# A three-layer feature-interaction network on one core: q of the first four chunks by pairs

## The chip, the cores and the metric

The kernel runs on one core of a Trainium2 chip. The metric is device time in microseconds (us), the median of several executions. Engines are named as the profile names them: PE (TensorE, matmul), PEld (its weight loads), DVE (VectorE), ACT (ScalarE), POOL (GpSimd), SP (the queue that issues most DMAs).

## The reference

```python
# x: (1024, 64, 16), W0, W1, W2: (128, 64*64)
h = x
for i in range(3):
    z = einsum('bfe,bge->bfge', x, h).reshape(B, 64 * 64, 16)
    y = einsum('oc,bce->boe', W[i], z) + b[i][None, :, None]
    x_i, h = (y[:, :64], y[:, 64:]) if i < 2 else (y, y)
    xs.append(x_i)
pooled = sum(concatenate(xs, axis=1), axis=2)      # over the 16 of e
out = pooled @ fc_w.T + fc_b                        # (1024, 1)
```

## The kernel before

All is fp32. The batch of 1024 is cut into 32 chunks of 32 rows. A chunk is a matrix of 64 features by 512 columns (32 rows times 16 of e).

**Algebra.** Products of x with itself are symmetric, so each pair of features (f, g) is made once, and the weights of (f, g) and (g, f) are added beforehand. The products of a chunk lie in 16 tiles z of 128 rows by 512 columns, made by VectorE in four instructions of four tiles each (`product`, L213, on line 217). The last group of four has one part (32 rows of its first tile) that holds squares, made by ScalarE (L222); the other 32 squares of a chunk are not in these tiles. From the same 16 tiles two 64-row results come: h1, the hidden half of layer 0, and q, a quadratic form of x that layer 2 and the output weights turn into (its weights m are built from W1 and W2 at run time). To q also belong the 32 other squares and a linear term, V1 x. The output of a chunk is the sum over e and features of uu0 = (h1 + bias) * q and uu1 = (V0 x + cx) * x, plus a constant.

**Weights.** `w_all` holds for each tile t 64 columns for h1, 64 for q, and 64 for h1 again (columns 128 to 191), so that an even chunk takes columns 0 to 127 (h1, q) and an odd one 64 to 191 (q, h1). `w_sq` is the same for the 32 other squares, four times below each other in row groups of 32. `v1w` is V1's weights, `bd` a block diagonal matrix of V0 (64 rows twice). q's weights come late: they are built by a chain of matmuls and sent through DRAM with DMAs into `ms`, and added by `q_weights`. So the first four chunks, `HEAD = [2, 3, 0, 1]`, are treated otherwise: h1 alone is made of them during the set-up, with `half_contract(c, 0, j)` (L286): 64 output rows, the columns 0 to 255 on one half of PE's columns and 256 to 511 on the other, side by side, into one accumulator of 128 rows by 256. `keep_h1` (L309) adds the squares to h1 of all four and ScalarE keeps h1 + bias in `hb`, in the same halves.

**q of the first four, before the change.** Chunks 0 and 1 are the last of the four; their z (`KEPT`) are still there when q's weights come, and `half_contract(c, 1, j)` makes their q at once (L545 to L548). Chunks 2 and 3 are loaded and multiplied a second time, within the main loop. The 17th tile, `zl`, made by ScalarE (`squares`, L224, and two copies in `last_tile`, L228), holds all 64 squares of the chunk and x itself; its weights in `w_all[:, NT]` are the first 32 squares' q weights, zeros, and V1. `half_contract(c, 1, NJ)` contracts it for each chunk. `v0x(k)` (L345) is a full 128x128 matmul of `bd` with the two chunks' x (`xx`). `factors` (L327) multiplies q with `hb`, in two pieces of 256 columns for each of these chunks.

**The other 28 chunks.** `contract(c, j)` (L254) makes h1 and q of a chunk with 16 full matmuls of 128x128 weights and 512 columns. After every second chunk of four, `contract_shared` (L263) adds what is missing to all four chunks: the squares, four matmuls of 32 rows in PE's four row groups, side by side; and for each pair of chunks V1 x and V0 x, four matmuls of 64 rows and 64 columns on the four quarters of PE.

**Order.** The program is in the order in which it is written (a manual schedule): each engine executes its instructions in that order, and waits by semaphores that are placed from the data and the buffers. The main loop (L629) goes over `order = [4, 5, 6, 7, 2, 3, 8, ..., 31]`; at step s it issues the loads and products of the chunk two steps ahead, contracts the present one, and has VectorE do the factors and sums of earlier ones. Chunks 4 and 5 are loaded before the loop. After chunk 4 the biases' constants and V0's weights are made (`biases`, `v0_weights`).

**Buffers.** x as loaded (`xa`, `xb`) has 3 buffers each, z has 12 (three chunks), `xx` 4, `zl` and the squares 4, `uu` 2. PSUM has 8 banks: tag "acc" 4, "y" 2, "set" 2. Buffers go round in turn.

Of the kernel before, what the change touches and what calls it, by code (L numbers as in the profile page):

```python
# [62 lines left out]
def cin_kernel(ctx, tc, xra, xrb, wh, w0r, w1h, w2t, wx1, wx0, vec, out):  # L63
# [11 lines left out]
    def const_tile(name, shape):  # L75
        return const.tile(shape, F32, tag=name, name=name)
# [49 lines left out]

    w_all = const_tile("w_all", [128, NT + 1, 192])
    w_sq = const_tile("w_sq", [128, 192])  # L130
    v1w = const_tile("v1w", [128, F])
    nc.gpsimd.memset(w_all[:, NT, :], 0.0)


    xas, xbs, zls, xxs, sqs = {}, {}, {}, {}, {}

    def load_xa(c, at=slice(0, NI)):
        if c not in xas or at.start == 0:
# [14 lines left out]
    def load_chunk(c):  # L153
        load_xa(c)
        load_xb(c)
# [40 lines left out]


    acc = const_tile("acc", [128, 2, NCH // 2, CB])
    hb = const_tile("hb", [128, NF, N // 2])
    accs, uus, zs, ys, parts = {}, {}, {}, {}, {}  # L200

    def new_acc(c, n=N, tag="acc"):
# [18 lines left out]
        if j == NJ - 1:  # L221
            nc.scalar.activation(zs[c, j][SQ, 0, :], xas[c][SQ, 0, :], AF.Square)  # L222

    def squares(c):  # L224
        zls[c] = xp.tile([128, N], F32, tag="zl", name=f"zl_{c}", bufs=4)
        nc.scalar.activation(zls[c][0:64], xas[c][0:64, 0, :], AF.Square)

    def last_tile(c):  # L228

        if c < FIRST:  # L230
            squares(c)
            nc.scalar.copy(zls[c][64:128], xas[c][64:128, 0, :])
        else:
            if c % 4 == 0:
                sqs[c // 4] = xp.tile([128, N], F32, tag="zl", name=f"sq_{c}", bufs=4)
            at = 32 * (c % 4)
            nc.scalar.activation(sqs[c // 4][at : at + 32], xas[c][0:32, 0, :], AF.Square)  # L237
        if c % 2 == 0:
            xxs[c // 2] = sp.tile([128, N], F32, tag="xx", name=f"xx_{c}", bufs=4)
        to = halves[c % 2]  # L240
        nc.scalar.copy(xxs[c // 2][to], xas[c][to, 0, :])  # L241

# [20 lines left out]
    def contract_shared(first):  # L263

        for r in range(4):
            c, at = first + r, slice(32 * r, 32 * r + 32)
            for acc_c, cols in pieces(c):
                nc.tensor.matmul(  # L268
                    acc_c, w_sq[at, w_cols(c)], sqs[first // 4][at, cols], start=(r >= 2),
                    stop=(r < 2), tile_position=(32 * r, 0),  # L270
                )
        for k in (first // 2, first // 2 + 1):
            ys[k] = ps.tile([128, N], F32, tag="y", name=f"y_{k}")
            for n in range(2):
                c, rows, q = 2 * k + n, halves[n], halves[1 - n]
                for acc_c, cols in pieces(c):
                    nc.tensor.matmul(  # L277
                        acc_c[q], v1w[rows], xxs[k][rows, cols], start=False, stop=(c % 4 < 2),
                        skip_group_check=True,
                    )  # L280
            for rows in halves:
                nc.tensor.matmul(ys[k][rows], bd[rows, rows], xxs[k][rows], start=True, stop=True)  # L282

    def half_contract(c, part, j):  # L286

        cols = slice(part * F, (part + 1) * F)
        for t in (NT,) if j == NJ else [j * NI + i for i in tiles(j)]:
            z = zls[c] if t == NT else zs[c, j][:, t % NI, :]  # L290
            for n in range(2):
                nc.tensor.matmul(  # L292
                    accs[c][halves[n]], w_all[:, t, cols], z[:, n * H2 : (n + 1) * H2],
                    start=(t == 0), stop=(t == NT),
                )


    sq_head = xp.tile([128, N], F32, tag="zl", name="sq_head", bufs=4)
    h1_accs = {}

    def head_square(c):
# [7 lines left out]
    def keep_h1():  # L309
        for r, c in enumerate(HEAD):  # L310
            at = slice(32 * r, 32 * r + 32)
            for n in range(2):
                nc.tensor.matmul(  # L313
                    h1_accs[c][halves[n]], w0ds[at], sq_head[at, n * H2 : (n + 1) * H2],
                    start=False, stop=True, tile_position=(32 * r, 64 * n),
                )
        for c in HEAD:
            nc.scalar.activation(
                hb[:, HEAD.index(c), :], h1_accs[c], AF.Identity, bias=bh1
            )  # L320

    def uu_tile(k):
# [4 lines left out]
    def factors(c, which=slice(0, 1)):  # L327

        uu = uu_tile(c // 2)[halves[c % 2], 0, :]
        if c in HEAD:  # L330
            for n in range(2):
                at = halves[n]
                nc.vector.tensor_tensor(
                    uu[:, n * H2 : (n + 1) * H2], accs[c][at], hb[at, HEAD.index(c), :], ALU.mult
                )
            return
        h = halves[c % 2]
        for acc_c, cols in pieces(c)[which]:
            q = sp.tile([128, N], F32, tag="q", name=f"q_{c}_{cols.start}")
            nc.scalar.copy(q[h, cols], acc_c[64 - h.start : 128 - h.start])  # L340
            nc.vector.scalar_tensor_tensor(  # L341
                uu[:, cols], acc_c[h], bh1[h], q[h, cols], ALU.add, ALU.mult
            )

    def v0x(k):  # L345
        ys[k] = ps.tile([128, N], F32, tag="y", name=f"y_{k}")
        nc.tensor.matmul(ys[k], bd, xxs[k], start=True, stop=True)  # L347

    def x_v0x(k):
        nc.vector.scalar_tensor_tensor(uu_tile(k)[:, 1, :], ys[k], cx, xxs[k], ALU.add, ALU.mult)  # L350
# [35 lines left out]
    nc.vector.memset(w0o[3][SQ, 0, :], 0.0)  # L386
    for j in (2, 3):
        h1_weights(j, w0o[j])
    half_contract(c0, 0, 0)


    head_acc(c1)
# [8 lines left out]
    product(c0, 3)  # L401
    load_chunk(c3)
    for j in range(1, NJ):
        half_contract(c0, 0, j)


    for j in range(NJ - 1):
# [13 lines left out]
            )  # L421
        nc.scalar.copy(v2r[:, n, :], pv)

    half_contract(c1, 0, 0)


    pt = ps.tile([128, F // 4, 4], F32, tag="y", name="pt")
# [2 lines left out]
        for to in halves:  # L430
            nc.tensor.matmul(pt[to, q, :], v2q[:, q, :], pick, start=True, stop=True)  # L431
    nc.scalar.copy(v2t, pt.rearrange("p q k -> p (q k)"))
    half_contract(c1, 0, 3)


    m_sb = z_tile("m_sb")
# [9 lines left out]
        nc.scalar.copy(m_sb[:, m, :], pms[m])  # L446

    for j in (1, 2):
        half_contract(c1, 0, j)

# [25 lines left out]
    for j in range(NJ):  # L476
        product(c2, j)
    for j in range(NJ):
        half_contract(c2, 0, j)


    ms = set_tile("ms").rearrange("p (v t g) -> p v t g", v=2, g=F)
# [31 lines left out]
    for j in range(NJ):  # L514
        product(c3, j)
    for j in range(NJ):
        half_contract(c3, 0, j)

    for j in range(1, NJ):
        for half in range(2):  # L520
# [14 lines left out]
    for j in range(NJ):  # L535
        q_weights(j)
    nc.vector.tensor_copy(w_all[SQ, (NJ - 1) * NI, 64:128], dg[SQ])
    nc.vector.tensor_copy(w_all[0:32, NT, 64:128], w_sq[0:32, 64:128])

    nc.scalar.copy(w_all[:, 0:NT, 128:192], w_all[:, 0:NT, 0:64])  # L540
    for to in (slice(0, 64), slice(128, 192)):
        nc.scalar.copy(w_sq[:, to], w0ds)


    for c in KEPT:  # L545
        new_acc(c, H2, "y")
        for j in range(NJ):
            half_contract(c, 1, j)  # L548

    made = set()  # L550

# [24 lines left out]
    for to in halves:  # L576
        for n in range(2):
            nc.vector.tensor_copy(v1w[to, 32 * n : 32 * n + 32], v1h[halves[n]])
    nc.scalar.copy(w_all[64:128, NT, 64:128], v1w[64:128])

    load_products(FIRST + 1)

# [12 lines left out]
    cst = const_tile("cst", [2, 1])  # L595

    def biases():
        pcx = ps.tile([128, 1], F32, tag="set", name="pcx")
        for to in halves:
            nc.tensor.matmul(pcx[to], v2t[0:64], bh2, start=True, stop=True)  # L600
        nc.scalar.copy(cx, pcx)
        pc = ps.tile([2, 1], F32, tag="set", name="pc")
        for j in range(2):
            nc.tensor.matmul(
                pc, fcol[:, j : j + 1].to_broadcast([128, 2]), bcol[:, j : j + 1],
                start=(j == 0), stop=(j == 1),
            )
        nc.scalar.activation(cst, pc, AF.Identity, bias=fcb, scale=float(E))


    NP = NCH // 2
    po = ps.tile([2, NP, CB], F32, tag="set", name="po")
    res = const_tile("res", [2, NP, CB])
    outs = out.rearrange("(k h b) o -> h k (b o)", h=2, b=CB)

# [12 lines left out]
    first, last = slice(0, NP - 1), slice(NP - 1, NP)  # L628
    for s, c in enumerate(order):  # L629
        k, head = c // 2, c in HEAD  # L630
        if s == 4:

            v0x(0)
            del uus[0]
            x_v0x(0)
            sums(0, of=slice(1, 2))
        if 0 < s < len(order) - 2:
            load_products(order[s + 2])
        if head or c % 4 < 2:
            new_acc(c, H2 if head else N)  # L640
        for j in range(NJ):
            if j == 2:
                if head and c % 2:
                    v0x(k)
            if head:
                half_contract(c, 1, j)
            else:
                contract(c, j)
        if head:
            half_contract(c, 1, NJ)  # L650
        elif c % 4 == 1:
            for n in (1, 2):
                new_acc(c + n)
            contract_shared(c - 1)
        if s == 0:
            for n in KEPT:
                half_contract(n, 1, NJ)
                factors(n)
            sums(0, of=slice(0, 1))
            biases()  # L660
            v0_weights()
            load_products(order[2], order[3])

        if head or c % 4 in (0, 3) and s:
            factors(order[s - 1])
            if order[s - 1] % 2:
                sums(order[s - 1] // 2)
        elif c % 4 == 2:
# [5 lines left out]
        if head and c % 2:  # L674
            x_v0x(k)


    sums(NP - 1, of=slice(1, 2))
# [85 lines left out]
```

## Time and profile before

| | |
|---|---|
| median of 5 runs | 492.80 us (492.74 to 492.88) |
| the profiled execution's own time | 493.02 us |
| its span, first to last instruction | 491.2 us |
| PE busy | 486.2 us (99%) |
| DVE busy | 369.1 us (75%) |
| ACT busy | 93.2 us (19%) |
| POOL busy | 11.4 us (2%) |
| granted PE clock | 1.00 |
| HBM | 159 GB/s over the span |

The profile is one execution of the program, taken by the hardware profiler. A span begins with the first instruction; what the time has beside it lies around it. An x with a count is a number of instructions as the hardware executed them: the trace shows an fp32 matmul as two passes, each with its weight load. Matmuls are pipelined, so durations of single passes overlap; the distance of their starts says what they cost. "128*64 128x256" is a matmul with weights of 128 rows and 64 columns and 256 columns streamed. The chain that ended last is followed back from the last instruction: at each step to what released it, or to the instruction before it on its engine.

### The profile page before, as it was taken

To read this page: it belongs to the slowest core of one execution; us is meant where nothing else is said; L and a number is where in the kernel's file an instruction comes from. 1 tells how busy PE (TensorE), PEld (TensorE's weight loads), DVE (VectorE), ACT (ScalarE), POOL (GpSimd) and SP (SyncE) were. 2 spreads that over 40 slices of the span, in tenths; PEclk is the share of its full clock that TensorE was granted. 3 is DMA by queue.
4 is the path that set the end of the run, shared out by engine and by line. 5 is a ranking of instruction groups with operands and counts; after the bars stand their busy time and mean duration, and the time that the engine had idled before them with its cause. 6 is when DMAs were issued, how large, how long until landed. Compare 5 with 4: busy or idle time off the path is not lost.

```text
span 491.2 us, 4356 instructions
## 1 busy us (share of the span) xinstructions
PE 486.2 (99%) x1820; PEld 229.7 (47%) x1820; DVE 369.1 (75%) x232; ACT 93.2 (19%) x162; POOL 11.4 (2%) x20
## 2 busy tenths in 40 slices
PE   9999999999999999999999999999999999999996
PEld 5656644344644344443444444443444434444474
DVE  4796799999889988898767777767878676780311
ACT  3323312022112221112111021112011121010001
POOL 5300000000000000000000000000000000000000
PEclk9999999999999999999999999999999999999999
DMA  8977974344444573545233444333344440000000
GB/s 333 423 243 202 422 323 171 145 197 172 172 171 171 189 280 118 209 187 216 79 109 154 172 171 171 133 133 109 137 172 171 171 156 16 0 0 0 1 1 0
DMA packets 14243, 78.60 MB, mean 160 GB/s; under 512 B 3756, under 2 KB 4428, under 8 KB 5200
## 3 DMA queue, kind: packets, MB, share of 16 engines
q1 hardware_dynamic: 13084, 77.05, 40.9%
q10 hardware_dynamic: 1140, 1.29, 1.0%
q8 instruction: 14, 0.23, 0.2%
q14 instruction: 5, 0.04, 0.0%
HBM read 76.69 MB, written 1.64 MB: 159 GB/s over the span
## 4 chain that ended last, share of the span: by engine, by line
PE 98%; DMA 1%; DVE 0%; ACT 0%; issue 0%
PE acc L258 79%; PE acc L292 12%; PE acc L277 3%; PE acc L268 2%; PE xp L186 1%; DMA xa<-in_xra 1%; PE po L617 0%; PE misc L105 0%; PE y L347 0%; PE pm L441 0%; PE pv L417 0%; PE pt L431 0%; PE y L282 0%; PE acc L313 0%; DVE uu L341 0%
## 5 line engine op out<-in xcount | busy, mean ns | idle before, releaser
L258 PE MATMUL acc<-z,w_all 128*128 128x512 f32 (+1 forms) x928 | 387.6, 579 | 0.0
L217 DVE TENSOR_TENSOR z<-xa,xb 128x2048 f32<-128x2048 f32 x128 | 287.9, 2286 | 48.3 <-PE acc L258 39.0
L258 PEld LDWEIGHTS acc<-z,w_all 128*128 128x128 f32 x928 | 175.4, 190 | 210.1 <-issue 206.5
L222 ACT ACTIVATE z<-xa 32x512 f32<-32x512 f32 x34 | 21.3, 626 | 322.5 <-DVE z L217 309.8
L341 DVE SCALAR_TENSOR_TENSOR uu<-acc,vs,q 64x512 f32<-64x512 f32 (+1 forms) x29 | 21.2, 732 | 61.3 <-ACT q L340 61.1
L292 PE MATMUL acc<-z,w_all 128*64 128x256 f32 x512 | 57.2, 381 | 0.0
L292 PEld LDWEIGHTS acc<-z,w_all 128*64 128x64 f32 x512 | 36.1, 137 | 21.8 <-issue 3.6
L340 ACT COPY q<-acc 64x512 f32<-64x512 f32 (+1 forms) x29 | 16.4, 565 | 36.5 <-PE acc L258 22.9
L354 DVE TENSOR_REDUCE acc<-uu 128x64 f32<-128x1024 f32 (+3 forms) x20 | 20.5, 1027 | 0.4
L241 ACT COPY xx<-xa 64x512 f32<-64x512 f32 x32 | 19.6, 613 | 0.5
L217 DVE TENSOR_TENSOR z<-xa,xp 128x2048 f32<-128x2048 f32 (+2 forms) x8 | 13.7, 1748 | 6.1 <-PE xp L186 6.1
L237 ACT ACTIVATE sq<-xa 32x512 f32<-32x512 f32 x28 | 17.6, 628 | 0.7
L282 PE MATMUL y<-xx,bd 64*64 64x512 f32 x56 | 13.6, 604 | 0.0
L277 PE MATMUL acc<-xx,v1w 64*64 64x512 f32 (+1 forms) x58 | 13.5, 587 | 0.0
L350 DVE SCALAR_TENSOR_TENSOR uu<-y,cx,xx 128x512 f32<-128x512 f32 x16 | 11.3, 745 | 0.3
L217 POOL TENSOR_TENSOR z<-xa,xb_gps 128x2048 f32<-128x2048 f32 x2 | 9.1, 4563 | 5.8 <-ACT xb_gps L370 3.4
L268 PE MATMUL acc<-sq,w_sq 32*128 32x512 f32 (+1 forms) x58 | 8.0, 623 | 0.0
L277 PEld LDWEIGHTS acc<-xx,v1w 64*64 64x64 f32 x58 | 3.6, 132 | 8.9 <-issue 8.8
L105 PE MATMUL misc<-bd 128*128 128x128 f32 x28 | 5.0, 347 | 1.0 <-POOL bd L99 1.0
L105 PEld LDWEIGHTS misc<-bd 128*128 128x128 f32 x28 | 4.5, 250 | 2.2 <-issue 1.2
L186 PE MATMUL xp<-xa,shift 64*64 64x512 f32 x32 | 5.2, 779 | 0.1
L268 PEld LDWEIGHTS acc<-sq,w_sq 32*128 32x128 f32 x58 | 2.6, 183 | 5.4 <-issue 5.3
(66 smaller groups left out, 64.0 us busy)
## 6 DMA issues: line engine op xcount, KB each, us to landing
xa<-in_xra SPq DMA_DIRECT2D x32, 1024.0 KB, 4.9
xb<-in_xrb SPq DMA_DIRECT2D x32, 1024.0 KB, 6.9
w<-in_w2t SPq DMA_DIRECT2D x2, 1024.0 KB, 10.1
xa<-in_xra SPq DMA_DIRECT2D x2, 768.0 KB, 6.5
w1s<-in_w1h SPq DMA_DIRECT2D x1, 1024.0 KB
w1x<-in_wx SPq DMA_DIRECT2D x1, 1024.0 KB, 8.7
w0x<-in_wx SPq DMA_DIRECT2D x1, 1024.0 KB, 8.3
w0t<-in_w0r SPq DMA_DIRECT2D x1, 768.0 KB, 6.5
```

The source lines that it names most:

```text
L217: engine.tensor_tensor(zs[c, j][:, at, :], xas[c][:, at, :], xbs[c][j].unsqueeze(1).to_broadcast([128, last - first, N]), ALU.mult,)
L222: nc.scalar.activation(zs[c, j][SQ, 0, :], xas[c][SQ, 0, :], AF.Square)
L237: nc.scalar.activation(sqs[c // 4][at : at + 32], xas[c][0:32, 0, :], AF.Square)
L241: nc.scalar.copy(xxs[c // 2][to], xas[c][to, 0, :])
L258: nc.tensor.matmul(acc_c, w_all[:, t, w_cols(c)], zs[c, j][:, i, cols], start=(t == 0 and c % 4 < 2), stop=(t == NT - NI and c % 4 >= 2),)
L268: nc.tensor.matmul(acc_c, w_sq[at, w_cols(c)], sqs[first // 4][at, cols], start=(r >= 2), stop=(r < 2), tile_position=(32 * r, 0),)
L277: nc.tensor.matmul(acc_c[q], v1w[rows], xxs[k][rows, cols], start=False, stop=(c % 4 < 2), skip_group_check=True,)
L282: nc.tensor.matmul(ys[k][rows], bd[rows, rows], xxs[k][rows], start=True, stop=True)
L292: nc.tensor.matmul(accs[c][halves[n]], w_all[:, t, cols], z[:, n * H2 : (n + 1) * H2], start=(t == 0), stop=(t == NT),)
L340: nc.scalar.copy(q[h, cols], acc_c[64 - h.start : 128 - h.start])
L341: nc.vector.scalar_tensor_tensor(uu[:, cols], acc_c[h], bh1[h], q[h, cols], ALU.add, ALU.mult)
L354: nc.vector.tensor_reduce(acc[rows, of, k, half], uus[k][rows, of, E * half.start : E * half.stop].rearrange("p k (b e) -> p k b e", e=E), ...
```

## The change

The first four chunks are finished as the others are, in part:

- **q by pairs.** `head_q(k, j)` takes the place of `half_contract(c, 1, j)`: chunk 2k goes to one half of PE's columns with all its 512 columns, chunk 2k+1 to the other, side by side, into one accumulator of 128 rows by 512 for the pair (`q_accs`). `half_contract` remains for h1 alone. Chunks 0 and 1 are contracted at the same place as before, tile by tile in turn. Chunks 2 and 3 are contracted together where chunk 3 was.
- **The rest once for all four.** `head_shared`, behind the q of chunks 2 and 3, adds V1 x and V0 x of both pairs on PE's quarters with `v1_v0` (the last part of `contract_shared`, taken out as a function), and the 32 squares in row groups from `sq_head`, which the set-up made for h1. The tile `zl`, its weights `w_all[:, NT]`, `squares` and `v0x` are gone.
- **hb** has the layout of `q_accs`, written in two pieces for each chunk; `factors` of these chunks is one instruction of 512 columns.
- **Order.** The products of chunks 2 and 3 are made in turn, the first two groups of both at step 2 and the others at step 3, instead of all of chunk 2 at step 2 and of chunk 3 at step 3. All factors, x V0 x and sums of the four chunks come at step 6 (chunk 8).
- **Buffers.** `xx` has 5 and `zl`/squares 3. `q_accs[0]` takes a "set" bank, `q_accs[1]` an "acc" bank; the two small tiles of `biases` share one bank, and the output's `po` is allocated after the loop.

```diff
-    w_all = const_tile("w_all", [128, NT + 1, 192])
+    w_all = const_tile("w_all", [128, NT, 192])
...
-    hb = const_tile("hb", [128, NF, N // 2])
+    hb = const_tile("hb", [128, NF // 2, N])
...
     def last_tile(c):
 
-        if c < FIRST:
-            squares(c)
-            nc.scalar.copy(zls[c][64:128], xas[c][64:128, 0, :])
-        else:
+        if c >= FIRST:
...
-            xxs[c // 2] = sp.tile([128, N], F32, tag="xx", name=f"xx_{c}", bufs=4)
+            xxs[c // 2] = sp.tile([128, N], F32, tag="xx", name=f"xx_{c}", bufs=5)
...
+    def v1_v0(k, at):
+        ys[k] = ps.tile([128, N], F32, tag="y", name=f"y_{k}")
+        for n in range(2):
+            c, rows, q = 2 * k + n, halves[n], halves[1 - n]
+            for acc_c, cols in at(c):
+                nc.tensor.matmul(
+                    acc_c[q], v1w[rows], xxs[k][rows, cols], start=False,
+                    stop=(c >= FIRST and c % 4 < 2), skip_group_check=True,
+                )
+        for rows in halves:
+            nc.tensor.matmul(ys[k][rows], bd[rows, rows], xxs[k][rows], start=True, stop=True)
...
-            nc.scalar.activation(
-                hb[:, HEAD.index(c), :], h1_accs[c], AF.Identity, bias=bh1
+            for n in range(2):
+                nc.scalar.activation(
+                    hb[halves[1 - c % 2], c // 2, n * H2 : (n + 1) * H2], h1_accs[c][halves[n]],
+                    AF.Identity, bias=bh1[halves[n]],
+                )
...
+    def head_q(k, j):
+        for i in tiles(j):
+            t = j * NI + i
+            for n in range(2):
+                nc.tensor.matmul(
+                    q_accs[k][halves[1 - n]], w_all[:, t, 64:128], zs[2 * k + n, j][:, i, :],
+                    start=(t == 0), stop=False,
+                )
+
+    def head_shared():
+
+        for k in q_accs:
+            v1_v0(k, lambda c: [(q_accs[c // 2], slice(0, N))])
+        for r, c in enumerate(HEAD):
+            at, q = slice(32 * r, 32 * r + 32), halves[1 - c % 2]
+            nc.tensor.matmul(
+                q_accs[c // 2][q], w_sq[at, 64:128], sq_head[at], start=False, stop=True,
+                tile_position=(32 * r, q.start),
+            )
...
         if c in HEAD:
-            for n in range(2):
-                at = halves[n]
-                nc.vector.tensor_tensor(
-                    uu[:, n * H2 : (n + 1) * H2], accs[c][at], hb[at, HEAD.index(c), :], ALU.mult
-                )
+            at = halves[1 - c % 2]
+            nc.vector.tensor_tensor(uu, q_accs[c // 2][at], hb[at, c // 2, :], ALU.mult)
...
-    for c in KEPT:
-        new_acc(c, H2, "y")
-        for j in range(NJ):
-            half_contract(c, 1, j)
+    q_accs[0] = ps.tile([128, N], F32, tag="set", name="q_0")
+    for j in range(NJ):
+        head_q(0, j)
...
-        if s == 4:
-
-            v0x(0)
-            del uus[0]
-            x_v0x(0)
-            sums(0, of=slice(1, 2))
-        if 0 < s < len(order) - 2:
+        if 0 < s < len(order) - 2 and s not in (2, 3):
             load_products(order[s + 2])
...
+        if s in (2, 3):
+
+            if s == 2:
+                for n in order[4:6]:
+                    load_chunk(n)
+                    last_tile(n)
+            for j in (0, 1) if s == 2 else (2, 3):
+                for n in order[4:6]:
+                    product(n, j)
+        if not head:
+            if c % 4 < 2:
+                new_acc(c)
+            for j in range(NJ):
                 contract(c, j)
-        if head:
-            half_contract(c, 1, NJ)
-        elif c % 4 == 1:
+        elif c % 2:
+            q_accs[k] = ps.tile([128, N], F32, tag="acc", name=f"q_{k}", bufs=4)
+            for j in range(NJ):
+                head_q(k, j)
+            head_shared()
...
         if s == 0:
-            for n in KEPT:
-                half_contract(n, 1, NJ)
-                factors(n)
-            sums(0, of=slice(0, 1))
             biases()
             v0_weights()
             load_products(order[2], order[3])
 
-        if head or c % 4 in (0, 3) and s:
+        if order[s - 1] in HEAD and not head:
+            for n in HEAD:
+                factors(n)
+                if n % 2:
+                    x_v0x(n // 2)
+                    sums(n // 2)
+        elif c % 4 in (0, 3) and s and order[s - 1] not in HEAD or c == HEAD[0]:
             factors(order[s - 1])
```

More of the change, by code (lines that the diff above doesn't have):

```diff
@@ L125, in cin_kernel @@
     nc.gpsimd.memset(ones[64:128, 1:2], 1.0)
-    w_all = const_tile("w_all", [128, NT + 1, 192])
+    w_all = const_tile("w_all", [128, NT, 192])
     w_sq = const_tile("w_sq", [128, 192])
     v1w = const_tile("v1w", [128, F])
-    nc.gpsimd.memset(w_all[:, NT, :], 0.0)
-    xas, xbs, zls, xxs, sqs = {}, {}, {}, {}, {}
+    xas, xbs, xxs, sqs = {}, {}, {}, {}
     def load_xa(c, at=slice(0, NI)):
@@ L222, in product @@
             nc.scalar.activation(zs[c, j][SQ, 0, :], xas[c][SQ, 0, :], AF.Square)
-    def squares(c):
-        zls[c] = xp.tile([128, N], F32, tag="zl", name=f"zl_{c}", bufs=4)
-        nc.scalar.activation(zls[c][0:64], xas[c][0:64, 0, :], AF.Square)
     def last_tile(c):
-        if c < FIRST:
-            squares(c)
-            nc.scalar.copy(zls[c][64:128], xas[c][64:128, 0, :])
-        else:
+        if c >= FIRST:
             if c % 4 == 0:
-                sqs[c // 4] = xp.tile([128, N], F32, tag="zl", name=f"sq_{c}", bufs=4)
+                sqs[c // 4] = xp.tile([128, N], F32, tag="zl", name=f"sq_{c}", bufs=3)
             at = 32 * (c % 4)
@@ L272, in contract_shared, with half_contract @@
         for k in (first // 2, first // 2 + 1):
-            ys[k] = ps.tile([128, N], F32, tag="y", name=f"y_{k}")
-            for n in range(2):
[L275 to L279, printed above, removed]
-                    )
[L281 to L290, printed above, removed]
+            v1_v0(k, pieces)
+    def v1_v0(k, at):
[9 more added lines that the diff above has]
+            nc.tensor.matmul(ys[k][rows], bd[rows, rows], xxs[k][rows], start=True, stop=True)
+    def half_contract(c, j):
+        for i in tiles(j):
+            t = j * NI + i
             for n in range(2):
                 nc.tensor.matmul(
-                    accs[c][halves[n]], w_all[:, t, cols], z[:, n * H2 : (n + 1) * H2],
-                    start=(t == 0), stop=(t == NT),
+                    accs[c][halves[n]], w_all[:, t, 0:64], zs[c, j][:, i, n * H2 : (n + 1) * H2],
+                    start=(t == 0), stop=False,
                 )
-    sq_head = xp.tile([128, N], F32, tag="zl", name="sq_head", bufs=4)
+    sq_head = xp.tile([128, N], F32, tag="zl", name="sq_head", bufs=3)
     h1_accs = {}
@@ L317, in keep_h1 @@
         for c in HEAD:
-            nc.scalar.activation(
-                hb[:, HEAD.index(c), :], h1_accs[c], AF.Identity, bias=bh1
+            for n in range(2):
[3 more added lines that the diff above has]
+                )
+    q_accs = {}
+    def head_q(k, j):
+        for i in tiles(j):
+            t = j * NI + i
+            for n in range(2):
+                nc.tensor.matmul(
+                    q_accs[k][halves[1 - n]], w_all[:, t, 64:128], zs[2 * k + n, j][:, i, :],
+                    start=(t == 0), stop=False,
+                )
[7 more added lines that the diff above has]
+                tile_position=(32 * r, q.start),
             )
@@ L330, in factors @@
         if c in HEAD:
-            for n in range(2):
-                at = halves[n]
-                nc.vector.tensor_tensor(
-                    uu[:, n * H2 : (n + 1) * H2], accs[c][at], hb[at, HEAD.index(c), :], ALU.mult
-                )
+            at = halves[1 - c % 2]
+            nc.vector.tensor_tensor(uu, q_accs[c // 2][at], hb[at, c // 2, :], ALU.mult)
             return
@@ L343, in factors @@
             )
-    def v0x(k):
-        ys[k] = ps.tile([128, N], F32, tag="y", name=f"y_{k}")
-        nc.tensor.matmul(ys[k], bd, xxs[k], start=True, stop=True)
     def x_v0x(k):
@@ L388, in cin_kernel @@
         h1_weights(j, w0o[j])
-    half_contract(c0, 0, 0)
+    half_contract(c0, 0)
     head_acc(c1)
@@ L403, in cin_kernel @@
     for j in range(1, NJ):
-        half_contract(c0, 0, j)
+        half_contract(c0, j)
     for j in range(NJ - 1):
@@ L422, in cin_kernel @@
         nc.scalar.copy(v2r[:, n, :], pv)
-    half_contract(c1, 0, 0)
+    half_contract(c1, 0)
     pt = ps.tile([128, F // 4, 4], F32, tag="y", name="pt")
@@ L432, in cin_kernel @@
     nc.scalar.copy(v2t, pt.rearrange("p q k -> p (q k)"))
-    half_contract(c1, 0, 3)
+    half_contract(c1, 3)
     m_sb = z_tile("m_sb")
@@ L448, in cin_kernel @@
     for j in (1, 2):
-        half_contract(c1, 0, j)
+        half_contract(c1, j)
     md = dr.tile([EXT, EXT, F], F32, tag="md", name="md")
@@ L478, in cin_kernel @@
     for j in range(NJ):
-        half_contract(c2, 0, j)
+        half_contract(c2, j)
     ms = set_tile("ms").rearrange("p (v t g) -> p v t g", v=2, g=F)
@@ L516, in cin_kernel @@
     for j in range(NJ):
-        half_contract(c3, 0, j)
+        half_contract(c3, j)
     for j in range(1, NJ):
@@ L537, in cin_kernel @@
     nc.vector.tensor_copy(w_all[SQ, (NJ - 1) * NI, 64:128], dg[SQ])
-    nc.vector.tensor_copy(w_all[0:32, NT, 64:128], w_sq[0:32, 64:128])
-    nc.scalar.copy(w_all[:, 0:NT, 128:192], w_all[:, 0:NT, 0:64])
+    nc.scalar.copy(w_all[:, :, 128:192], w_all[:, :, 0:64])
     for to in (slice(0, 64), slice(128, 192)):
         nc.scalar.copy(w_sq[:, to], w0ds)
-    for c in KEPT:
-        new_acc(c, H2, "y")
-        for j in range(NJ):
-            half_contract(c, 1, j)
+    q_accs[0] = ps.tile([128, N], F32, tag="set", name="q_0")
+    for j in range(NJ):
+        head_q(0, j)
     made = set()
@@ L578, in cin_kernel @@
             nc.vector.tensor_copy(v1w[to, 32 * n : 32 * n + 32], v1h[halves[n]])
-    nc.scalar.copy(w_all[64:128, NT, 64:128], v1w[64:128])
     load_products(FIRST + 1)
@@ L597, in biases @@
     def biases():
-        pcx = ps.tile([128, 1], F32, tag="set", name="pcx")
+        pb = ps.tile([128, 2], F32, tag="set", name="pb")
+        pcx, pc = pb[:, 0:1], pb[0:2, 1:2]
         for to in halves:
             nc.tensor.matmul(pcx[to], v2t[0:64], bh2, start=True, stop=True)
-        nc.scalar.copy(cx, pcx)
-        pc = ps.tile([2, 1], F32, tag="set", name="pc")
         for j in range(2):
@@ L607, in biases @@
             )
+        nc.scalar.copy(cx, pcx)
         nc.scalar.activation(cst, pc, AF.Identity, bias=fcb, scale=float(E))
     NP = NCH // 2
-    po = ps.tile([2, NP, CB], F32, tag="set", name="po")
     res = const_tile("res", [2, NP, CB])
@@ L630, in cin_kernel @@
         k, head = c // 2, c in HEAD
-        if s == 4:
-            v0x(0)
-            del uus[0]
-            x_v0x(0)
-            sums(0, of=slice(1, 2))
-        if 0 < s < len(order) - 2:
-            load_products(order[s + 2])
[L639 to L644, printed above, removed]
-            if head:
-                half_contract(c, 1, j)
-            else:
-                contract(c, j)
-        if head:
-            half_contract(c, 1, NJ)
-        elif c % 4 == 1:
+        if 0 < s < len(order) - 2 and s not in (2, 3):
+            load_products(order[s + 2])
+        if s in (2, 3):
[10 more added lines that the diff above has]
+            for j in range(NJ):
+                contract(c, j)
+        elif c % 2:
[3 more added lines that the diff above has]
+            head_shared()
+        if c % 4 == 1 and not head:
             for n in (1, 2):
@@ L667, in cin_kernel @@
                 sums(order[s - 1] // 2)
-        elif c % 4 == 2:
+        elif c % 4 == 2 and not head:
             factors(c - 2)
@@ L673, in cin_kernel @@
             sums(k - 1)
-        if head and c % 2:
-            x_v0x(k)
+    po = ps.tile([2, NP, CB], F32, tag="set", name="po")
     sums(NP - 1, of=slice(1, 2))
```

## The prediction

> **What bounds the kernel now.** I read the page's table of busy shares first, to see which engine could set the time at all:
>
> ```profile
> PE 486.2 (99%) x1820; PEld 229.7 (47%) x1820; DVE 369.1 (75%) x232; ACT 93.2 (19%) x162; POOL 11.4 (2%) x20
> ```
>
> PE is busy in 99% of the span. A share is only an average, so next comes the chain of waits, in order of time, through the stretch that the change rewrites. Its columns are start, length, and what ran (a count x is of passes: the trace shows every fp32 matmul as two).
>
> ```profile
> 27.58 17.42 PE acc L292 x160
> 45.00 0.62 PE acc L313 x16
> 45.62 13.96 PE acc L292 x128
> 59.58 13.93 PE acc L258 x32
> 73.51 1.01 PE acc L292 x8
> 74.53 0.21 PE pcx L600 x4
> ...
> 88.84 1.07 PE acc L268 x8
> 89.91 0.58 PE acc L277 x2
> 90.49 0.01 PE y L282 x2
> ...
> 119.45 0.86 PE y L347 x2
> 120.31 10.94 PE acc L292 x100
> 131.25 1.06 PE y L347 x2
> 132.31 4.04 PE acc L292 x36
> 136.34 27.66 PE acc L258 x64
> ...
> 166.96 55.13 PE acc L258 x128
> ```
>
> No other engine and no wait stands between these pieces: each begins where the one before it ends. So a microsecond of PE work that goes is a microsecond of the end, as long as VectorE, which makes the products, stays ahead. The granted clock is 1.00 in every stretch, so all passes are at one speed.
>
> Third is the timeline of VectorE, because its share is 95% and more in parts of the stretch from 52 to 178 us. Columns: start, length, line, form, count, and idle time before with its releaser.
>
> ```profile
> 66.30 8.90 DVE L217 TENSOR_TENSOR z<-xa,xb 128x2048 f32<-128x2048 f32 x4
> 75.11 1.72 DVE L333 TENSOR_TENSOR uu<-acc,hb 64x256 f32<-64x256 f32 x4
> 82.90 26.51 DVE L217 TENSOR_TENSOR z<-xa,xb 128x2048 f32<-128x2048 f32 x12
> 114.73 8.89 DVE L217 TENSOR_TENSOR z<-xa,xb 128x2048 f32<-128x2048 f32 x4
> 126.95 8.89 DVE L217 TENSOR_TENSOR z<-xa,xb 128x2048 f32<-128x2048 f32 x4
> ```
>
> These are the products of chunk 5, of chunks 6, 7 and 2, of chunk 3, and of chunk 8; one takes 2.2 us. Chunk 8's first is ready at 129.2 and PE asks for it at 136.3: 7 us of cover. Chunk 5's first is ready at 68.5 and wanted at 74.8: 6 us, the thinnest of these.
>
> **Prices of a pass.** From 32 passes in 13.93 and 128 in 55.13, one full pass of 512 columns is (55.13 - 13.93) / 96 = 0.429 us, and entering a stage of another shape costs 0.20. From 128 half-wide passes (64 pairs) in 13.96 and 160 (80 pairs) in 17.42, a pair of 256 columns side by side is 3.46 / 16 = 0.216, the entry 0.12.
>
> **The change part by part.**
>
> *The last tile of q goes.* It was eight matmuls of 256 columns, 16 passes on zl. Those of chunks 0 and 1 are the piece at 73.51: 1.01 us, four pairs and their entry. Those of chunks 2 and 3 are eight of the 136 passes of L292 between 120.31 and 136.34.
>
> *q of chunks 2 and 3 by pairs.* Before, from the end of chunk 7 to the start of chunk 8: 136.34 - 119.45 = 16.89 us, with 64 pairs of z, four of zl and two full V0 x matmuls. After, 32 pairs of 512 columns. The trace of before has no such pair of this shape; its nearest rows are the quarter passes of 512 columns, four side by side, that follow each other by 0.43 (0.42 and 0.01 in the chain). So 32 x 0.429 + 0.12 = 13.85 us. The work is the same number of columns; the 0.11 that it is shorter than 64 x 0.216 is a smaller share of starts. Ends: no gain over 64 x 0.216 + 0.12 = 13.96, and 13.80.
>
> *V1 x, V0 x and the squares, once for four chunks.* V1 x is a matmul of 64 rows on one quarter, V0 x of both halves the others: just what the shared step of the later chunks does from 89.91 to 91.79, 1.88 us for two pairs. The squares are four matmuls in row groups: 1.07 at 88.84, there 128 columns wide, here 64. Together 2.95 us. In sum 13.85 + 2.95 = 16.80 where 16.89 was: 0.09 less. The V0 x (0.86 and 1.06) and zl's passes pay for what is added.
>
> *q of chunks 0 and 1* in the stretch from 45.62: 13.96 becomes 13.85, 0.11 less. The products and the weights that it asks for are there sooner than it wants them: the fourth group of weights is written at 46.5, and each group of tiles is now reached twice as late.
>
> *Sum:* 1.01 + 0.09 + 0.11 = 1.2 us less on PE. Ends: 0.9, if the wide pairs gain nothing and the row groups at 64 columns pay 0.1 more for the changes of shape; 1.35, if they pay less.
>
> *ScalarE.* The eight activations and copies for zl go, 0.62 each. hb is written in eight pieces of 256 columns for four (four took 1.57), so 1.6 more at 45.6, while 2.5 of zl goes there. At 19% busy it lies beside PE. Chunk 5's load waits for the copy of xx of chunk 0: about 0.4 us later than 48.98, for a product that starts at 66.3.
>
> *VectorE's order.* The factors and sum of chunks 0 and 1 (1.72 and 0.69 at 75.11) leave their place, so the products of 6 and 7 come 2.4 us sooner, up to 98.3. Then the products of 2 and 3 alternate, four before the factors of chunks 4 and 5 and four after. The four before carry no square on ScalarE, so the 1.30 us for which the factors waited on ScalarE's copy go too. I add the durations up: four products to 107.2, factors, x V0 x and sum 4.0 us, four products to 120.0, chunk 6's factor after its ScalarE wait to 122, chunk 8's products from there, the first ready at 124.3. PE wants the pairs of 2 and 3 from 118.3 in steps of 3.5, the last group at 128.8; the last product and its square are there at 120.7: 8 us of cover. Chunk 8 is wanted at 135.1: 10.8.
>
> *The loads.* On SP's queue the order stays. Chunk 3's buffer comes free with chunk 6's last product at 90.0; median landing is 4.9 and 6.9 us (xa and xb), so 97.9 against a product at 100.4. w0x can start at 50 for 54.4, because its buffer is given back after the first group of pairs, and chunk 6 behind it. Both pass nothing that is wanted before 66.
>
> *The new block.* After chunk 10's products, about 152, VectorE makes all four factors, two x V0 x and two sums: 6 x 0.74 + 2 x 1.21 = 6.9 us (the 64x512 form with a scalar is the nearest: 0.73). Chunk 10's copy of xx on ScalarE waits for that block (its buffer was chunk 0's), and behind the copy is chunk 10's square: ready at 159, wanted by PE at 178. The accumulators that chunks 8 to 11 share are wanted at 163 and V0 x's at 164; the block gives them back by 153.4 and 157.6. 6 us of cover; if it were gone, PE would wait for what is missing.
>
> **A rule against it.** The three stretches with 64 rows or 32 now put two row tiles into one PSUM bank at a time: V1 x of both chunks of a pair, and two of the four squares. Until now V1 x wrote two banks; but V0 x wrote both its row halves to one:
>
> ```profile
> 90.32 0.60 PE L277 MATMUL acc<-xx,v1w 64*64 64x512 f32 x2
> 90.33 0.60 PE L282 MATMUL y<-xx,bd 64*64 64x512 f32 x2
> 90.75 0.60 PE L277 MATMUL acc<-xx,v1w 64*64 64x512 f32 x2
> ```
>
> Both V0 x passes start within 0.01 us of V1's, and the next group follows 0.43 later. So rows say that the tiles overlap; what they do not show is two row tiles that accumulate in one bank. The page "TensorEngine Tiling (Array Packing)" of the Trainium skill states, under "Restrictions and Gotchas", that different row tiles cannot access the same PSUM bank simultaneously. By it V0 x itself would have been twice as long, which the trace contradicts; by it the sum would be some 1.4 us slower than before. I go by the row.
>
> **The rivals.**
>
> *Row tiles of one bank take turns when they accumulate* (slower). V1 x would need two more passes for each pair, 4 x 0.429 = 1.72, and the squares two more, 0.86: 2.58 more against 1.2 less, so 1.4 slower, 494.2. It decides as soon as over 1.2 us of that is lost, nearly half. Against it: V0 x above. For it: only that accumulation is new.
>
> *VectorE or a load comes late* (same or slower). Chunk 3 is now needed at 100.4 for 117, 2.5 us after its landing. A load that is 5 us late moves VectorE by 2.5 and PE not at all; past 2.5 + 8 us each one costs its length. xb's median would have to more than double. Nothing lost unless it does; a load 12 us late would give 493.1.
>
> *The gain is smaller than the measurement can tell.* Wide pairs at 0.436 instead of 0.429 eat 0.2 twice, and each change of shape costs up to 0.2: 1.2 becomes 0.6, or 492.2. For it: the entries of 0.12 to 0.20 are all that I have on changes of shape. Against: both old and new have the same number of these.
>
> *The pairs do not run side by side,* as each reads another z (not what the change says). Then 64 passes more at 0.429, twice 13.7: 520. The 256-wide passes of before already stream different columns side by side, so I give it almost nothing.
>
> **How the numbers follow.** The profiled execution took 493.02 us for a span of 491.2, 1.8 around it; the median, 492.80, is 0.2 below. The span goes to 490.0, the profiled time to 491.8, and the median to 492.8 - 1.2 = 491.6. A measurement of this kernel can tell about 0.2%, 0.99 us, from no change: faster is below 491.81. Forecast 0.80 (491.4 to 491.9; about one in ten of it ends above 491.81), small gain 0.08, row tiles 0.06, late operands 0.05, no overlap 0.01. Faster 0.72; within 0.2% 0.16 (0.08 of the forecast's edge, the small gain's 0.08); slower 0.12. The range 491.4 to 492.3 takes in the forecast and the small gain, less a little at the low end.
>
> **What would show it.** The group acc<-zl is gone; q<-z,w_all 128*64 128x512 stands at 128 passes, in two pieces of the chain of 13.85; no V0 x 128*128 is left. Between chunks 4 and 5 only the constants' 0.38 remains. Chunk 8 starts 1.2 us sooner than 136.34, and from there every piece has its old length. A wait of PE on VectorE or ScalarE before chunk 8 would make the cover wrong; a shared step of over 3.5 us after q of 2 and 3, the row tiles; pieces of 14.1 and more, the pass's price.

## The result, and the profile after

The changed kernel takes 491.72 us (median of 24 runs) where the kernel before takes 492.92 in 42 runs on the same chips: a ratio of 0.9978, 95% interval 0.9972 to 0.9983. That is 1.1 to 1.2 us less. The profiled execution took 491.7 us for a span of 489.9, which was 491.2.

The busy shares of the profile come first, then the chain of waits in order of time (start, length, what ran, passes); line numbers are those of the changed kernel.

```profile
PE 484.8 (99%) x1696; PEld 219.3 (45%) x1696; DVE 368.4 (75%) x226; ACT 90.5 (18%) x157; POOL 11.2 (2%) x19
```

```profile
45.53 13.88 PE q L323 x64
59.42 13.93 PE acc L250 x32
73.35 0.21 PE pb L608 x4
73.56 0.17 PE pb L610 x4
...
90.61 27.66 PE acc L250 x64
118.27 13.88 PE q L323 x64
132.16 0.58 PE q L272 x2
132.73 0.01 PE y L277 x2
132.75 0.42 PE q L272 x2
...
134.03 1.02 PE q L334 x8
135.05 27.66 PE acc L250 x64
...
165.66 55.13 PE acc L250 x128
```

Between chunk 4 and the constants (`pb`) the piece of 1.01 us on zl is gone. The two stretches of q are 13.88 us each, in half as many passes. Behind the second stand the shared step's quarters, 1.87 us (132.16 to 134.03), and the squares, 1.02. Chunk 8 starts at 135.05 where it was 136.34, and from there every piece has its old length. PE has no wait in the whole stretch.

VectorE's timeline after (start, length, line, form, count) shows the cover, that is, how long a thing is ready before PE asks for it: the second four products of chunks 2 and 3, chunk 8's products, and the last x V0 x of the new block.

```profile
111.20 8.89 DVE L216 TENSOR_TENSOR z<-xa,xb 128x2048 f32<-128x2048 f32 x4
...
122.06 8.88 DVE L216 TENSOR_TENSOR z<-xa,xb 128x2048 f32<-128x2048 f32 x4
...
156.73 0.75 DVE L360 SCALAR_TENSOR_TENSOR uu<-y,cx,xx 128x512 f32<-128x512 f32 x1
```

Chunks 2 and 3 are complete at 120.1, chunk 8's first product is there at 124.3 and PE asks for it at 135.0. The bank of the last x V0 x comes back at 157.5; PE writes it at 164.6.

### The profile page after: what moved, and what is told of

Its sections match the earlier page's. It is cut to its first block, busy times and chain, and to the rows that moved or that the text cites. A ratio compares the mean times of both kernels' runs of the same rounds, so it can differ in the third digit from the quotient of the medians.

```text
span 489.9 us, 4089 instructions
## 1 busy us (share of the span) xinstructions
PE 484.8 (99%) x1696; PEld 219.3 (45%) x1696; DVE 368.4 (75%) x226; ACT 90.5 (18%) x157; POOL 11.2 (2%) x19
## 3 DMA queue, kind: packets, MB, share of 16 engines
q10 hardware_dynamic: 1140, 1.29, 1.0%
## 4 chain that ended last, share of the span: by engine, by line
PE 97%; DMA 1%; DVE 1%; SPq 0%; ACT 0%; issue 0%; ACTq 0%
PE acc L250 79%; PE q L323 6%; PE acc L284 5%; PE acc L272 3%; PE acc L260 2%; DMA w0t<-in_w0r 1%; DVE z L216 0%; PE po L623 0%; PE pm L451 0%; PE pv L427 0%; PE q L272 0%; PE pt L441 0%; PE xp L185 0%; PE q L334 0%; PE y L277 0%
## 5 line engine op out<-in xcount | busy, mean ns | idle before, releaser
L284 PE MATMUL acc<-z,w_all 128*64 128x256 f32 x256 | 28.7, 381 | 0.0
L323 PE MATMUL q<-z,w_all 128*64 128x512 f32 x128 | 27.9, 594 | 0.0
L284 PEld LDWEIGHTS acc<-z,w_all 128*64 128x64 f32 x256 | 17.9, 137 | 11.1 <-issue 2.5
L323 PEld LDWEIGHTS q<-z,w_all 128*64 128x64 f32 x128 | 9.0, 137 | 18.3 <-issue 17.5
L277 PE MATMUL y<-xx,bd 64*64 64x512 f32 x64 | 15.5, 603 | 0.0
```

The costliest lines, as they stand in the source:

```text
L284: nc.tensor.matmul(accs[c][halves[n]], w_all[:, t, 0:64], zs[c, j][:, i, n * H2 : (n + 1) * H2], start=(t == 0), stop=False,)
L323: nc.tensor.matmul(q_accs[k][halves[1 - n]], w_all[:, t, 64:128], zs[2 * k + n, j][:, i, :], start=(t == 0), stop=False,)
```

## The experiments

The theory: PE alone sets the end here, so the gain is the columns that PE no longer streams, 1.01 of it between chunks 4 and 5, and everything else that the change moves is covered. The rivals tested: that the number of matmuls counts, that VectorE (busy without a gap from 52 to 110 us) sets the pace, and that the new order of the products bought the gain. All medians are in us.

**The wide pairs alone**, on the kernel before:

```diff
-    for c in KEPT:
-        new_acc(c, H2, "y")
-        for j in range(NJ):
-            half_contract(c, 1, j)
+    q_accs[0] = ps.tile([128, N], F32, tag="y", name="q_0")
+    for j in range(NJ):
+        head_q(0, j)          # chunks 0 and 1, 512 columns each; zl contracted likewise, later
...
```

`hb` in its new layout and the factors of 512 columns come with it.

> The kernel before with the wide pairs alone: q of each pair of chunks in 32 pairs of 512 columns, the last tile zl and the full V0 x matmuls kept. If the gain is that of columns not streamed, little of it comes from here: each pair of chunks spares 0.07 to 0.11 us of starts, together 0.15 to 0.2, so 492.7 where the kernel before has 492.9, and the piece of zl of chunks 0 and 1 still takes 1.0. If what counts is the number of matmuls (128 passes fewer, half of the narrow ones), most of the 1.2 us is here: 491.9 or less.

Measured: 492.68 against 492.94, ratio 0.9997 (0.9988 to 1.0006). In its chain, q of chunks 0 and 1 and zl's piece:

```profile
45.41 13.88 PE q L331 x64
59.30 13.93 PE acc L258 x32
73.23 1.01 PE q L331 x4
```

The wide stretch takes the 13.88 of the changed kernel, and zl's piece takes 1.01 in half as many passes. A pass costs its columns; how many instructions they come in is worth 0.08 in 14 us here (13.88 for 13.96). No gain that can be measured comes from the pairs by themselves.

**Without zl for chunks 0 and 1**, on the kernel before:

```diff
...
             for n in KEPT:
-                half_contract(n, 1, NJ)
                 factors(n)
```

The output then lacks the 32 squares and V1 x of these two chunks.

> The kernel before without the contraction of zl for chunks 0 and 1 (16 passes in the trace's count halves to eight in one piece): their 32 squares and V1 x are left out of q. If PE sets the end everywhere, the 1.01 us piece goes from the end in full: 491.9. If VectorE, busy without a gap from 52 to 110 us, sets the pace behind it, less than 0.5 arrives: 492.4 or more, and a wait of PE shows before chunk 8.

Measured: 491.82 against 492.94, ratio 0.9978 (0.9968 to 0.9987); the span 490.1 for 491.2. From its chain:

```profile
59.45 13.93 PE acc L258 x32
...
73.76 13.93 PE acc L258 x32
...
135.19 27.66 PE acc L258 x64
```

Between chunks 4 and 5 only the constants' 0.38 is left. Chunk 8 starts at 135.19 for 136.34, and PE does not wait. The piece goes from the end in full, behind a VectorE that works without a gap. This is nearly all of what the change brings. (The piece has eight passes; the 16 are those of all four chunks.)

**The changed kernel with the old order of products:**

```diff
-        if 0 < s < len(order) - 2 and s not in (2, 3):
+        if 0 < s < len(order) - 2:
             load_products(order[s + 2])
```

with the alternating products of steps 2 and 3 taken out.

> The kernel after with the order of loads and products of before: all of chunk 2 at step 2, all of chunk 3 at step 3. If the order is cover alone, the time stays: 491.7 (within 0.2), PE without a wait; VectorE gets back its 1.3 us wait for the copy of chunk 4's q, so chunk 8's products start about 1 us later with 9 us of cover left. If alternating the products bought the gain, this is 492.5 or more.

Measured: 491.79, ratio 0.9977 (0.9967 to 0.9987). From its chain:

```profile
134.97 27.66 PE acc L250 x64
```

VectorE has its wait of 1.30 us for ScalarE back, and chunk 8's first product starts at 122.34, where it was 122.06 in the changed kernel; chunk 8 itself starts at 134.97, no later. The alternating order is cover and brings nothing by itself.

**How deep is the cover?** Idle multiplications on a spare tile, ahead of chunk 8's products:

```diff
+        if s == 4:
+            spare = w1x.rearrange("p (k c) -> p k c", c=64)
+            for _ in range(8):        # 4 in cover_9, 6 in cover_14
+                nc.vector.tensor_tensor(
+                    spare, spare, fcr[:, 0:64].unsqueeze(1).to_broadcast([128, 32, 64]), ALU.mult
+                )
```

With eight:

> The kernel after with eight idle multiplications of 128x2048 on a spare tile ahead of chunk 8's products, 8 x 2.28 = 18.3 us on VectorE. By the cover counted (chunk 8's first product at 124.3, wanted at 135.0: 10.7 us) PE waits 18.3 - 10.7 = 7.6 us ahead of chunk 8 and the time is 499.3. If VectorE's load were what sets the end in this stretch, all 18.3 arrive: 510. If the products ahead of PE make up for more than the first tile, less than 7.

Measured: 502.41, 10.7 more than the changed kernel and not 7.6. The wait ahead of chunk 8 is about as counted, but behind it the contraction of chunks 8 and 9 is longer than it was (PE's timeline, first of the changed kernel, then of this run; in brackets the idle time before and who ended it):

```profile
134.98 27.73 PE L250 MATMUL acc<-z,w_all 128*128 128x512 f32 x64
```

```profile
142.17 30.54 PE L250 MATMUL acc<-z,w_all 128*128 128x512 f32 x64 [7.36 <-DVE z L216]
```

Of what is missing, 2.8 us stand here as passes at a lower clock. By stretches (start:end, length, busy time of PE, PEld, DVE, ACT, POOL, granted clock, DMA):

```profile
138.00:140.00 2.00, 0.00 (x0) 0.00 (x0) 2.00 (x2) 0.00 (x0) 0.00 (x0) 0.50 0.00 0
144.00:146.00 2.00, 2.00 (x4) 0.93 (x3) 2.00 (x2) 0.00 (x0) 0.00 (x0) 0.50 0.00 0
148.00:150.00 2.00, 2.00 (x6) 0.95 (x5) 0.72 (x1) 1.21 (x2) 0.00 (x0) 1.00 0.00 0
```

The clock fell to 0.50 while PE waited and stayed there for the first passes, which follow each other by 0.85 us, not 0.43. Another 0.7 is in the shared step behind chunk 9. Whether the end would have come sooner without the slow passes is answered further down, with the run of six.

With four:

> The same with four idle multiplications, 9.1 us on VectorE. By the cover counted, 10.7 us, nothing is lost: 491.7, chunk 8's first product ready at 133.4, 1.6 us before PE wants it. If VectorE sets the pace here, 9.1 are lost: 500.8.

Measured: 493.03, ratio 1.0003 to before (0.9994 to 1.0012): the whole gain of the change lost, where I had expected no loss. Chunk 8 did not wait. I had counted one cover and forgotten the other, which the prediction has: the new block. PE's timeline at the shared step of chunks 8 to 11, and the block's last x V0 x on VectorE:

```profile
164.37 1.02 PE L272 MATMUL acc<-xx,v1w 64*64 64x512 f32 x4
166.07 1.08 PE L277 MATMUL y<-xx,bd 64*64 64x512 f32 x4 [0.67 <-DVE uu L360]
167.07 33.31 PE L250 MATMUL acc<-z,w_all 128*128 128x512 f32 x77
```

```profile
165.26 0.75 DVE L360 SCALAR_TENSOR_TENSOR uu<-y,cx,xx 128x512 f32<-128x512 f32 x1
```

V0 x of the second pair waits until VectorE has read the bank that V0 x of chunks 0 and 1 was in. Its passes then run by themselves instead of beside V1 x, so the wait shows as 0.67 of idle time but costs 1.7: chunk 10 starts at 167.07 instead of about 165.3.

**The same load with the block in another order**, to see whether it is the place in VectorE's line:

```diff
-            for n in HEAD:
+            for n in HEAD[:2]:
                 factors(n)
-                if n % 2:
-                    x_v0x(n // 2)
-                    sums(n // 2)
+            x_v0x(1)
+            x_v0x(0)
+            sums(1)
+            for n in KEPT:
+                factors(n)
+            sums(0)
```

> cover_9 lost 1.4 us although chunk 8 did not wait: PE waited at 164.4 for the bank of V0 x of chunks 10 and 11, which VectorE gave back with x V0 x of chunks 0 and 1, at 166.03, the last but one of the new block at chunk 8's step. Here the same four idle multiplications, and the block in another order: both x V0 x straight behind the factors of chunks 2 and 3, ahead of the first sum and the other factors (1.22 + 2 x 0.69 = 2.6 us less). If the block's place in VectorE's line is the cause, the bank is free at 163.4 and nothing is lost: 491.7. If VectorE's load as such costs 1.3, it stays 493.0.

Measured: 491.67. VectorE has as much to do, 9.2 us more than in the changed kernel, and none of it is seen. Both x V0 x now end at 163.06:

```profile
161.65 1.41 DVE L360 SCALAR_TENSOR_TENSOR uu<-y,cx,xx 128x512 f32<-128x512 f32 x2
```

So it is one release, not the load. **With six:**

> Six idle multiplications, 13.9 us with their starts. Ahead of chunk 8 PE waits 7.36 - 4.6 = 2.75 us, if cover is counted as in cover_18. The total loss by the block: VectorE is 13.9 later and x V0 x of chunks 0 and 1 had some 7.2 us of cover, so 6.7 are lost: 498.4. If the wait of 7.36 us in cover_18, behind which the granted clock was 0.50 and passes took 0.85 us, was long enough to lose the clock and one of 2.75 is not, the passes of chunk 8 keep to 0.43 here and PE waits again at V0 x, by 3.5 to 4 us. If a shorter wait loses the clock too, the passes of chunk 8 are slow again for 5 us.

Measured: 497.82, 6.1 lost. PE's timeline and the stretches behind the wait:

```profile
137.69 29.43 PE L250 MATMUL acc<-z,w_all 128*128 128x512 f32 x64 [2.79 <-DVE z L216]
```

```profile
137.00:138.00 1.00, 0.30 (x1) 0.30 (x2) 1.00 (x2) 0.00 (x0) 0.00 (x0) 1.00 0.00 0
139.00:140.00 1.00, 1.00 (x2) 0.37 (x2) 1.00 (x2) 0.00 (x0) 0.00 (x0) 0.50 0.00 0
142.00:143.00 1.00, 1.00 (x4) 0.45 (x3) 1.00 (x2) 0.00 (x0) 0.00 (x0) 0.99 0.00 0
```

A wait of 2.79 us loses the clock too, though it falls only after PE has started again (at 137.69) and is back sooner: 29.43 for 27.73, 1.7 us where it was 2.8. The 1.7 does not move the end, because V0 x's bank comes later still. With six and with eight, this is PE at V0 x of the second pair, and in the run with eight also VectorE at what gives the bank back:

```profile
170.85 1.07 PE L277 MATMUL y<-xx,bd 64*64 64x512 f32 x4 [0.79 <-DVE uu L360]
```

```profile
175.32 1.08 PE L277 MATMUL y<-xx,bd 64*64 64x512 f32 x4
176.33 23.87 PE L250 MATMUL acc<-z,w_all 128*128 128x512 f32 x55
```

```profile
174.52 0.75 DVE L360 SCALAR_TENSOR_TENSOR uu<-y,cx,xx 128x512 f32<-128x512 f32 x1
```

With eight the bank is free at 174.52 + 0.75 = 175.27 and V0 x starts at 175.32. VectorE's timeline has no wait for PE from the idle multiplications to there, so at full clock PE would have waited 2.8 us longer at this bank, and chunk 10 would have started at 176.33 all the same (165.59 in the changed kernel, 10.7 sooner). The 10.7 is therefore the block's cover running out, and the slow clock lies inside it. All three runs lose the time added on VectorE (9.2, 13.9 and 18.6 us with their starts) less 7.8 to 7.9 us, whatever PE does in between; from the bank's release to its use there are 7.2 us in the profile of the changed kernel and 8.3 in that of its repeat, below.

**The changed kernel again, and a version with fewer changes of shape.** In the second, `head_squares` stands behind the row groups of chunks 4 to 7, both `q_accs` in the "set" banks:

```diff
+        if first == FIRST:
+            head_squares()
         for k in (first // 2, first // 2 + 1):
             v1_v0(k, pieces)
...
+    for to in halves:                       # in the set-up, behind the matmuls of pm
+        nc.tensor.matmul(misc[to, 0:1], v2t[0:64], bh2, start=True, stop=True)
...
         if j == 2:
+            biases()                        # what is left of it: the output's constant
             pool(first, 1)
...
```

> The changed kernel itself, beside the others on one chip: 491.7, span 489.9.

> The kernel after with fewer changes of shape on PE: the heads' squares join the row groups of chunks 4 to 7 (both q accumulators in the two set banks), the bias product with V2 follows the set-up's matmuls on quarters, and the output's constant stands ahead of the pooling matmuls, which have its shape. The work is the same. From the rows of after: the squares' piece of 1.02 has 0.86 of passes, so 0.16 goes, and the constants' 0.38 between chunks 4 and 5 becomes some 0.15 elsewhere, so 0.2 goes: 491.3 to 491.4 where after has 491.7, a span of 489.5. If changes of shape cost nothing and only columns count: 491.7.

Measured: 491.66 (ratio 0.9979, 0.997 to 0.9988) for the changed kernel; 491.17 (0.9967, 0.9954 to 0.9979) for the other, the fastest of all: its slowest run (491.33) is below the other's fastest (491.44). The size is near what I expected, the split is not:

```profile
59.52 27.66 PE acc L250 x64
87.18 1.07 PE acc L260 x8
88.25 1.02 PE q L339 x8
```

The squares still take 1.02: going from 32 rows by 128 columns to 32 by 64 is a change of shape like any other, so moving them spared nothing. The constants spared more. Their 0.38 is gone, and chunks 4 and 5 run as one stage, 27.66 for 2 x 13.93: 0.58 in all, and 0.20 of it is the second entry. Given back are 0.06 in the set-up (from the start of pm's matmuls to the start of the next stage 1.94 for 1.88) and 0.10 ahead of the pooling (1.86 for 1.76); the sum, 0.42, is the 0.4 by which the span is shorter. The page "TensorEngine Tiling (Array Packing)" of the Trainium skill says under "Tiling Modes" that a change of mode drains the engine. The rows show 0.1 to 0.2 us for a change of shape; that a drain is what takes it, they do not show.

## Why the prediction was right

Forecast 491.6, measured 491.72; faster by more than 0.2%, as the likeliest case said, though only just: by 0.22%, with an interval of 0.17% to 0.28% that reaches under the line.

- **zl for chunks 0 and 1:** 1.01 forecast. 1.01 is gone from the chain, and its removal alone made the time 1.1 us shorter.
- **q of chunks 0 and 1:** 13.85 forecast, 13.88 measured. Less by 0.08 for 0.11.
- **q of chunks 2 and 3 and the shared step:** 16.80 forecast for 16.89, measured 135.05 - 118.27 = 16.78. The quarters take 1.87 (1.88 forecast), the squares 1.02 (1.07).
- **Sum:** 1.01 + 0.08 + 0.11 = 1.20, forecast 1.2. Chunk 8 stands 1.29 sooner; the last 0.09 was there at 45.5 us already, ahead of the changed work on PE. In PE's timeline that point lies between 45.21 and 45.56 over the runs here (45.46 and 45.55 in these two), so this part may be chance.
- **VectorE's order:** the products of 2 and 3 complete at 120.1 (forecast 120.0), chunk 8's first at 124.3 (124.3), the block 151.9 to 158.7 (6.9 us forecast). The 1.30 us wait for ScalarE at the factors of chunks 4 and 5 is gone.
- **Row tiles of one bank:** the quarters of V1 x, now accumulating two and two in one bank, follow each other by 0.43, as before with two banks. The four squares, two to a bank, take 1.02 for two steps of 0.43 and their entry. The rival is excluded. The page "TensorEngine Tiling (Array Packing)" of the Trainium skill states under "Restrictions and Gotchas" that different row tiles cannot access the same PSUM bank simultaneously; these rows, whose tiles of one bank write different halves of its partitions, do not show that.

Two side steps were wrong and cost nothing. w0x was to start at 50 us; it started at 56.0, later than before. PE gives the z of chunks 0 and 1 back in turn now, and the wait of SP's queue ended with the third of the four groups of pairs, not with the first. I had counted buffers by the order in which they were taken; the trace fits the order in which they come free. And ScalarE's eight pieces of hb took 3.86 us, not 3.1: 0.47 is what one takes by itself. So chunk 5's load was issued at 50.05, 1.1 us later than before and not 0.4; its product at 66.5 did not wait.

One cover was named but not put in order: I gave the block 6 us and chunk 8 10.8, and used the larger in the expectation of the run with four idle multiplications. The smaller decides.

## What to carry to other kernels

Where the chain is one engine from end to end, price a change in that engine's streamed columns, read from the steps of its starts, and add the changes of shape, 0.1 to 0.2 us each here. Regrouping the same columns into fewer instructions was worth 0.08 us in 14. For everything that is moved off that engine, list every buffer that it gives back, with the time at which it is wanted again: the thinnest of these is the cover, and it can lie 30 us behind the edit. When a block of work is put together, put first in it what releases something.

## What the runs showed of the hardware

A wait of PE slowed the stage behind it. After 7.36 us without work the granted clock was 0.50 (it fell some 2.8 us after PE's last pass, by a mean of 0.81 between 137 and 138 us), and the passes behind the wait came every 0.85 us until it was back at 1.00, 5.7 us after PE had started again: the stage took 2.8 us more. After 2.79 us the clock fell as well, for 3.4 us, and the stage took 1.7 us more; with 0.67 us of idle time it stayed at 1.00. In neither of the two runs did this move the end, as V0 x's bank was later. The page "TensorE: Matmul & The Clock Gate" of the Trainium skill, under "What's actually happening", states that the default state is throttled and that an idle window of about 3.4 us brings it back. The halving agrees with these runs; a wait that the profile gives as 2.79 us is shorter than that figure and was enough here. In the shorter case the fall came about 0.9 us after PE had started again (a mean clock of 0.80 between 138 and 139 us); why it came then was not tested.
